# A seven-product matmul kernel on one core: the first loads spread over three DMA queues, the first matmuls narrower, and three small pieces of vector work cut in halves

## The chip, the cores and the metric

The kernel runs on one core of one Trainium2 chip. The metric is the device time of one execution in microseconds (us), the median of several runs. The core has five engines that run side by side, each through its own instructions in order: PE (TensorE, the matmuls; "PEld" in the profile is its loading of weights), DVE (VectorE), ACT (ScalarE), POOL (GpSimd) and SP (SyncE, which here only issues DMA transfers). SP, ACT and POOL each have a DMA queue. Operands lie in SBUF, matmul results in eight PSUM banks.

## What is computed

The input `x` is 1024 x 512, `weight` is 64 x 512 x 512, `lin_w` is 512 x 512. Cut to what matters:

```python
out_lin = x @ lin_w.T + lin_b
xv = jnp.einsum('bf,efm->bem', x, weight)
zp = jnp.einsum('bf,efm->bem', jnp.square(x), jnp.square(weight))
out = out_lin + 0.5 * jnp.sum(jnp.square(xv) - zp, axis=1)
```

Since the sum over e of `x^2 @ w_e^2` is `x^2 @ sum_e w_e^2`, the kernel needs one matmul of `x` with every `w_e`, whose result is squared and summed, and besides only sums of squares of the weights.

## The kernel before, in words

**The work.** Every matmul is done as seven products of blocks in place of eight (a Strassen-like scheme). `x` transposed is cut in four quads `A11, A12, A21, A22` (half of the batch by half of the features), and from them come seven left operands: `A11`, `A12`, `A22` themselves and `R5, R6, R7, R3`, which DVE makes as differences (`x_sum`, line 520). A right matrix is cut in quads too. The products carry the numbers 1 to 7; number 1 needs `A11`, number 2 `A12`, number 4 `A22`, number 5 `R5`.

**Stage one, the linear term** (lines 572 to 656). PE works through products 1, 2, 4, 5, 6, 3, 7 of `x` and `lin_w`, in plain fp32, four matmuls of 512 columns each (`one_level`). The right operands are the quads of `lin_w`, called `lw0` and `lw1` (row r) with column c 0 or 1, and four sums of them, `lt` 1 to 4 (`column_sums`, line 534): sum 1 is lw0 c0 + lw0 c1, sum 2 is sum 1 + lw1 c1, sum 3 is lw0 c1 + lw1 c1, sum 4 is lw1 c0 + sum 2. Product 4 takes sum 4, product 5 sum 1, product 6 sum 2, product 7 sum 3. In front of all that stand two matmuls of zeros (line 607): they need no load and keep PE at work from the start.

**The first loads** (lines 488 to 513). SP's queue brings `x` in pieces of 256 KB, each half a quad (k 0 or 1 of it): `A11` k 0 and 1, `A12` 0 and 1, `A22`, `A21`, then the bias. ACT's queue brings `lin_w`: `lw0` c0 in two pieces of 128 KB, `lw1` c0, `lw0` c1, `lw1` c1 in pieces of 256 KB. POOL's queue brings nothing then. Behind these stand the first weights on SP's queue. A piece is awaited by its own semaphore; there are eight for the transfers of SP and ACT, so a ninth transfer waits until the first has landed.

**Stage two, the weights** (from line 952). 32 blocks h of the weights, each with four quads `w11, w12, w21, w22` loaded as 512 KB, go through products 1, 6, 2, 3, 7, 5, 4. Each operand of a product is split into three pieces `H, L, K` (`split`, line 710), and a product is three passes of fp32r matmuls of 512 columns (line 782), with ACT, DVE and POOL making the pieces, adding, squaring and summing. For the sums of squares, ACT squares each weights' quad and DVE sums it (`w_squares`, line 703): one `ACTIVATE` and one `TENSOR_REDUCE` of 128 x 1024 for each. `IN_HALVES` (line 40) names the blocks whose `w21` is loaded as two transfers of 256 KB.

**Stage three** (from line 974) multiplies the squares of `x` with the sums of squares (line 936) and stores the result.

**The order.** No engine's order is written down. Every operation is entered in a plan (class `Plan`, line 84) with a cost on its engine, its reads and writes; loads have assumed times of landing (`landing`, line 485). PE's order is fixed by keys. `Plan.order` (line 180) lays out the others by how late each may come, in 60 rounds with random shifts, and the best round is emitted. So a changed cost or time of landing anywhere gives a new order of ACT, DVE, POOL and SP everywhere.

**Names in the listings.** `w11_1` holds `A11`, `w12_1` `A12`, `w22_1` `A22`, `sq_0` `A21`, `p5_0` `lw0`, `p1_1` `lw1`, `p5_1` the sums 1 and 2, `p5_2` the sums 3 and 4, `p1_0` `R5`, `w_0` `R7`, `sq_1` `R6`, `w_1` `R3` (the table `home`); the profile leaves the numbers out, so `xT` into `w` is a load of `A11`, `A12` or `A22`, and `lin_wT` into `p` one of `lin_w`. `X1H, X1L, X1K` and so on are the three pieces of a left operand.

## Time and profile before

| what | us |
|---|---|
| median of 3 runs | 1276.41 (1275.95 to 1278.27) |
| the profiled execution, time | 1276.26 |
| its span in the trace | 1274.4 |
| PE busy | 1270.1 |
| DVE, POOL, ACT busy | 1105.6, 1051.9, 1022.4 |

The span runs from the first to the last instruction in the trace; 1.86 us of the profiled execution's time lie outside it. The trace gives each instruction's start, its busy time, and, where its engine stood idle before it, what ended the wait; a group's row gives how many there are and the mean of one. "Us to landing" is from the start of the instruction that issues a transfer to the arrival of its last byte. A matmul of fp32 appears as two records and two loads of weights.

### The profile page before, as it was taken

How to read it: one execution, taken by the hardware profiler on the slowest of the kernel's cores; microseconds unless marked ns; L12 is line 12 of the kernel's file. 1: busy time of each engine (PE TensorE's matmuls, PEld its weight loads, DVE VectorE, ACT ScalarE, POOL GpSimd, SP SyncE). 2: the span in 40 equal slices, each digit the busy share in tenths (PEclk: the TensorE clock that was granted, in tenths of full speed). 3: DMA queues.
4: the chain of work that ended last, by engine and by line, in shares of the span. 5: the costliest groups of instructions: out<-in, count | busy, mean ns of one | idle time of the engine just before them, and what ended most of it. 6: DMA issues, size and time to landing. Idle time of an engine off the chain costs nothing.

```text
span 1274.4 us, 15633 instructions
## 1 busy us (share of the span) xinstructions
PE 1270.1 (100%) x5532; PEld 1036.8 (81%) x5532; DVE 1105.6 (87%) x959; ACT 1022.4 (80%) x1080; POOL 1051.9 (83%) x532
## 2 busy tenths in 40 slices
PE   9999999999999999999999999999999999999998
PEld 4888888888888888888888888888888888888887
DVE  6899998888888898888898888898888888888987
ACT  7788987788877788877788877788887788887991
POOL 2998898888898888898888898888888888888884
PEclk9999999999999999999999999999999999999999
DMA  8776655445655455655545655545654546665553
GB/s 247 191 167 168 136 107 141 120 96 141 149 109 143 120 119 130 153 114 135 128 98 131 149 115 141 140 102 123 154 123 125 134 99 139 149 127 126 141 123 101
DMA packets 69597, 170.49 MB, mean 134 GB/s; under 512 B 23088, under 2 KB 24880, under 8 KB 69520
## 3 DMA queue, kind: packets, MB, share of 16 engines
q0 software_dynamic: 20240, 72.49, 33.3%
q1 hardware_dynamic: 47744, 95.31, 22.7%
q10 hardware_dynamic: 1536, 1.70, 0.4%
q8 instruction: 43, 0.70, 0.2%
q14 instruction: 34, 0.28, 0.1%
HBM read 158.73 MB, written 8.13 MB: 131 GB/s over the span
## 4 chain that ended last, share of the span: by engine, by line
PE 100%; DVE 0%; DVEq 0%; issue 0%
PE bank L782 96%; PE bank L936 2%; PE bank L590 1%; PE bank L579 1%; PE bank L607 0%; DVE T L1027 0%; DVEq L1069 0%
## 5 line engine op out<-in xcount | busy, mean ns | idle before, releaser
L446 POOL TENSOR_TENSOR pK<-pH,pL 128x1024 fp32r<-128x1024 f32 x225 | 593.0, 2640 | 171.2 <-PE bank L782 160.9
L453 DVE TENSOR_REDUCE acc<-sq 128x16 f32<-128x1024 f32 x256 | 310.3, 1214 | 48.2 <-ACT sq L428 47.1
L428 ACT ACTIVATE sq<-bank 128x1024 f32<-128x1024 f32 x256 | 261.4, 1021 | 102.7 <-PE bank L782 64.8
L446 POOL TENSOR_TENSOR pL<-T,pL 128x1024 fp32r<-128x1024 f32 x95 | 257.7, 2713 | 2.8 <-DVE X5K L434 1.2
L434 DVE SCALAR_TENSOR_TENSOR bank<-bank,w 128x1024 f32<-128x1024 f32 x192 | 235.0, 1224 | 26.0 <-PE bank L782 25.8
L440 DVE TENSOR_TENSOR w<-bank,p 128x1024 f32<-128x1024 f32 x128 | 156.1, 1219 | 47.8 <-PE bank L782 47.4
L434 DVE SCALAR_TENSOR_TENSOR bank<-bank,p 128x1024 f32<-128x1024 f32 x128 | 154.0, 1224 | 25.9 <-ACT p L428 23.0
L446 POOL TENSOR_TENSOR pL<-w,pL 128x1024 fp32r<-128x1024 f32 x64 | 171.5, 2679 | 1.3 <-ACT pL L428 0.5
L428 ACT ACTIVATE pL<-T 128x1024 fp32r<-128x1024 f32 x95 | 100.4, 1057 | 68.7 <-issue 44.4
L453 DVE TENSOR_REDUCE w_sum<-wsq 128x16 f32<-128x1024 f32 x128 | 154.2, 1205 | 0.0
L428 ACT ACTIVATE wsq<-w 128x1024 f32<-128x1024 f32 x128 | 135.7, 1060 | 2.7 <-DVE w_sum L453 2.7
L428 ACT ACTIVATE bank<-bank 128x1024 f32<-128x1024 f32 x128 | 130.1, 1017 | 8.8 <-PE bank L782 8.8
L428 ACT ACTIVATE pH<-w 128x1024 fp32r<-128x1024 f32 x129 | 136.7, 1059 | 0.0
L428 ACT ACTIVATE p<-bank 128x1024 f32<-128x1024 f32 x128 | 127.2, 1024 | 0.7 <-PE bank L782 0.7
L465 POOL DMA_DIRECT2D T<-weight x94 | 99.2, 1071 | 7.8 <-POOL pL L446 7.8
L428 ACT ACTIVATE pL<-w 128x1024 fp32r<-128x1024 f32 x66 | 70.0, 1061 | 43.0 <-PE bank L782 24.1
L428 ACT ACTIVATE pH<-T 128x1024 fp32r<-128x1024 f32 x96 | 101.1, 1053 | 0.0
L434 DVE SCALAR_TENSOR_TENSOR pL<-pH,w 128x1024 fp32r<-128x1024 f32 x63 | 95.6, 1517 | 0.4 <-ACT pH L428 0.4
L782 PE MATMUL bank<-pH,X4H 128*128 128x512 f32 x256 | 79.6, 392 | 0.0
L782 PE MATMUL bank<-pH,X1H 128*128 128x512 f32 x256 | 79.2, 391 | 0.0
L782 PE MATMUL bank<-pL,X4L 128*128 128x512 f32 x256 | 79.0, 390 | 0.0
L782 PE MATMUL bank<-pL,X1L 128*128 128x512 f32 x256 | 78.8, 389 | 0.0
(148 smaller groups left out, 2515.9 us busy)
## 6 DMA issues: line engine op xcount, KB each, us to landing
w<-weight SPq DMA_DIRECT2D x114, 512.0 KB, 6.3
T<-weight POOLq DMA_DIRECT2D x94, 512.0 KB, 6.0
w<-weight POOLq DMA_DIRECT2D x32, 512.0 KB, 8.4
T<-weight SPq DMA_DIRECT2D x31, 512.0 KB, 4.5
w<-weight SPq DMA_DIRECT2D x28, 256.0 KB, 5.7
accd<-turned SPq DMA_DIRECT2D x60, 32.0 KB, 5.1
w<-xT SPq DMA_DIRECT2D x6, 256.0 KB, 4.9
lind<-accd POOLq DMA_DIRECT2D x3, 512.0 KB, 5.2
```

The lines of the kernel that those rows point to most:

```text
L428: nc.scalar.activation(o, i, func, bias=bias, scale=scale)
L434: return nc.vector.scalar_tensor_tensor(o, i, scalar, j, ALU.mult, op)
L440: return (nc.vector.tensor_sub if sub else nc.vector.tensor_add)(o, a, b)
L446: return (nc.gpsimd.tensor_sub if sub else nc.gpsimd.tensor_add)(o, a, b)
L453: lambda _: nc.vector.tensor_reduce(o, i.rearrange("p a (m e) -> p a m e", e=E), axis=AX.X, op=ALU.add),
L465: {POOL: 1.05}, lambda _: nc.gpsimd.dma_start(o, i, accum_op=ALU.add),
L579: return nc.tensor.matmul(buf[bank[u]], b[:, k, ts(u, P)], a[:, k, :], start=first and k == 0, stop=k == KH - 1, skip_group_check=True,)
L590: made = nc.tensor.matmul(buf[bank[u]], b[:, k, ts(u, P)], a[:, k, :], start=first and k == 0, stop=k == KH - 1, skip_group_check=True,)
L782: made = nc.tensor.matmul(buf[bank, j], buf[x][:, k, ts(2 * half + j, P)], buf[w][:, k, :], start=first and k == 0, stop=k == KH - 1, skip ...
L936: made = nc.tensor.matmul(buf[bank[u]], w[:, k, (2 * c + u) * P:(2 * c + u + 1) * P], x[:, k, :], start=fresh and z == 0 and i == which[0] ...
```

## The change

- `A11` k 1 and the whole of `A12` (512 KB, one transfer) go to POOL's queue. SP's queue has `A11` k 0, now in two transfers of 256 columns (128 KB each), then `lw0` c1, then `A22`, `A21` and the bias. ACT's queue has `lw0` c0, cut by columns u 0 and 1 (128 KB each, both k), then `lw1` c0 and c1.
- The four matmuls of product 1's first step (k 0; u 0 and 1) become four of 256 columns in place of two of 512, so that the first needs one half of `A11` k 0 and one half of `lw0` c0.
- Of the two matmuls of zeros the second has 256 columns in place of 512.
- Sums 2 and 4 are made in two halves (u 0 and 1) each, and sum 4 is entered ahead of sum 3.
- `w21`'s square and its sum are done in two halves for blocks 8 to 27, and blocks 12 and 13 join those whose `w21` is loaded in halves.
- The assumed times of landing are new, and with them the whole order.

```diff
-IN_HALVES = tuple((h, "w21") for h in range(14, 28))
+IN_HALVES = tuple((h, "w21") for h in range(12, 28))
+SUMS_IN_HALVES = tuple((h, "w21") for h in range(8, 28))
...
-    load_x("A11", 0, 4.2)
-    load_lw(nc.scalar, [0], 0, 4.3)
-    load_lw(nc.scalar, [1], 0, 5.1)
-    load_x("A11", 1, 5.9)
-    load_lw(nc.scalar, [2, 3], 0, 7.0)
-    load_x("A12", 0, 7.4)
-    load_lw(nc.scalar, [0, 1], 1, 8.8)
-    load_x("A12", 1, 8.5)
-    load_lw(nc.scalar, [2, 3], 1, 9.6)
+    load_x(nc.gpsimd, "A11", [1], 4.5)
+    load_x(nc.gpsimd, "A12", [0, 1], 6.8)
+    for z, at in enumerate((3.2, 4.0)):
+        nc.sync.dma_start(buf["A11"][:, 0, ts(z, H // 2)], x_src[:, 0, z * (H // 2):(z + 1) * (H // 2)])
+        landing(("A11", 0, z), at)
+        nc.scalar.dma_start(buf["lw0"][:, :, ts(z, P)], lw_src[:, :KH, ts(z, P)])
+        for k in range(KH):
+            landing(("lw0", k, 0, z), at + 0.2)
...
+    load_lw(nc.scalar, 1, 0, 5.8)
+    load_lw(nc.sync, 0, 1, 5.8)
+    load_lw(nc.scalar, 1, 1, 7.0)
     for at, (n, k) in enumerate((("A22", 0), ("A22", 1), ("A21", 0), ("A21", 1))):
-        load_x(n, k, 10.1 + 0.7 * at)
+        load_x(nc.sync, n, [k], 7.4 + 0.8 * at)
...
             (1, q[0, 0], q[0, 1], needs[0, 0] + needs[0, 1]),
             (2, t[1], q[1, 1], names[1] + needs[1, 1]),
+            (4, q[1, 0], t[2], needs[1, 0] + names[2]),
             (3, q[0, 1], q[1, 1], needs[0, 1] + needs[1, 1]),
-            (4, q[1, 0], t[2], needs[1, 0] + names[2]),
         ):
-            add(t[k], x, y, r, names[k])
+            if k in (1, 3):
+                dve(t[k], x, y, False, r, names[k], 512, True)
+                continue
+            for u in range(2):
+                o, x_u, y_u = (z[:, :, ts(u, P)] for z in (t[k], x, y))
+                reads = tuple(n for n in r if n[0] != "lt" or n[2] == u)
+                dve(o, x_u, y_u, False, reads, names[k][u:u + 1], 256, True)
...
+                if p == 1 and not k:
+                    for z in range(2):
+                        def emit(_, u=u, z=z):
+                            return nc.tensor.matmul(
+                                buf[bank[u]][:, ts(z, H // 2)], b[:, 0, ts(u, P)],
+                                a[:, 0, ts(z, H // 2)], start=first, stop=False,
+                                skip_group_check=True,
+                            )
...
-            plan.add({PE: 2 * WHOLE}, emit, a_names + b_names + (bank[u],), (bank[u],),
-                     key=key + 0.1 * u)
+            reads = a_names + tuple(n for n in b_names if n[0] != "lt" or n[2] == u)
+            plan.add({PE: 2 * WHOLE}, emit, reads + (bank[u],), (bank[u],), key=key + 0.1 * u)
...
-    for u in range(2):
+    for u, n in enumerate((N, N // 2)):
         nc.tensor.matmul(
-            buf[f2[u]], zero[:, 0:P], zero, start=True, stop=True, skip_group_check=True
+            buf[f2[u]][:, :n], zero[:, 0:P], zero[:, :n], start=True, stop=True,
+            skip_group_check=True,
         )
-    plan.add({PE: 3.4}, None, (), tuple(f2), key=-2000)
+    plan.add({PE: 3.3}, None, (), tuple(f2), key=-2000)
...
-        act(buf[sq], buf[n], AF.Square, (n,), (sq,))
         m = (h // NCB) * MG + (2 * col + h % NCB) * MI
-        reduce(w2_sum[:, ts(row, KH), m:m + MI], buf[sq], (sq,), (("w2", row, m),))
+        if (h, q) not in SUMS_IN_HALVES:
+            act(buf[sq], buf[n], AF.Square, (n,), (sq,))
+            reduce(w2_sum[:, ts(row, KH), m:m + MI], buf[sq], (sq,), (("w2", row, m),))
+            return
+        part = (sq, "second")
+        for k, reads, o in ((0, (n,), sq), (1, (n, sq), part)):
+            act(buf[sq][:, k], buf[n][:, k], AF.Square, reads, (o,), 512)
+        for k, reads in ((0, (sq,)), (1, (sq, part))):
+            at = row * KH + k
+            reduce(w2_sum[:, at:at + 1, m:m + MI], buf[sq][:, k:k + 1], reads, (("w2", row, m),), 512)
```

How the instructions stand on the engines is shown at three places. First SP, at the start of the program, before (`w11_1` is `A11`, `w12_1` `A12`, `w22_1` `A22`, `sq_0` `A21`, `p5_0` `lw0`):

```order
L490 DMA w11_1_87<-xT 128x512 x2
L490 DMA w12_1_89<-xT 128x512 x2
L490 DMA w22_1_92<-xT 128x512 x2
L490 DMA sq_0_104<-xT 128x512 x2
L512 DMA bias_121<-lin_b 128x4
```

and SP there after the change:

```order
L505 DMA w11_1_87<-xT 128x256 x2
L498 DMA p5_0_111<-lin_wT 128x2x256
L492 DMA w22_1_92<-xT 128x512 x2
L492 DMA sq_0_104<-xT 128x512 x2
L517 DMA bias_121<-lin_b 128x4
```

`A22`, fifth on SP's queue before, is now fourth, behind 512 KB in place of 1 MB; `A11` k 1 and `A12` have left the queue, and `lw0` c1 has come onto it from ACT's.

Second POOL, at the start of the program, before (`X2L` and `X2K` are pieces of `A12`, the additions are done by the transfers; `pK` is the first operand of the weights that POOL makes):

```order
L1062 MEMSET const-uint8-127 128x1
L1069 UNCONDITIONAL_BRANCH
L465 DMA X2L_69<-w12_1_89 128x1024
L465 DMA X2K_70<-X2L_69 128x1024
L446 ISA
L446 TENSOR_TENSOR pK_0_101<-pH_0_95,pL_0_98 128x1024
```

and POOL there after the change:

```order
L1094 MEMSET const-uint8-127 128x1
L1101 UNCONDITIONAL_BRANCH
L492 DMA w11_1_87<-xT 128x512
L492 DMA w12_1_89<-xT 128x2x512
L466 DMA X2L_69<-w12_1_89 128x1024
L466 DMA X2K_70<-X2L_69 128x1024
L447 ISA
L447 TENSOR_TENSOR pK_0_101<-pH_0_95,pL_0_98 128x1024
```

The loads of `A11` k 1 and of `A12` stand in front of what POOL's queue began with.

Third DVE, from its first instruction on, before (`p5_1` holds the sums 1 and 2, `p5_2` 3 and 4):

```order
L440 TENSOR_TENSOR X1L_66<-w11_1_87,X1H_65 128x1024
L440 TENSOR_TENSOR p5_1_112<-p5_0_111 128x512
L440 TENSOR_TENSOR p5_1_112<-p5_1_112,p1_1_108 128x512
L440 TENSOR_TENSOR p5_2_113<-p1_1_108,p5_1_112 128x512
L440 TENSOR_TENSOR p5_2_113<-p5_0_111,p1_1_108 128x512
L434 SCALAR_TENSOR_TENSOR X1K_67<-X1H_65,X1L_66 128x1024
L440 TENSOR_TENSOR p1_0_107<-w22_1_92,sq_0_104 128x1024
```

and DVE there after the change:

```order
L441 TENSOR_TENSOR X1L_66<-w11_1_87,X1H_65 128x1024
L441 TENSOR_TENSOR p5_1_112<-p5_0_111 128x512
L441 TENSOR_TENSOR p5_2_113<-p5_0_111,p1_1_108 128x512
L441 TENSOR_TENSOR p5_1_112<-p5_1_112,p1_1_108 128x2x128 x2
L441 TENSOR_TENSOR p5_2_113<-p1_1_108,p5_1_112 128x2x128 x2
L435 SCALAR_TENSOR_TENSOR X1K_67<-X1H_65,X1L_66 128x1024
L441 TENSOR_TENSOR p1_0_107<-w22_1_92,sq_0_104 128x1024
```

The rows are the sums in turn: 1, 2, 4, 3 before; now 1, then 3, then the halves of 2, then the halves of 4.

More of the change, by code (lines that the diff above doesn't have):

```diff
@@ L448, in pool, with reduce @@
         plan.add({POOL: 0.1 + 2.24 * size / 1024}, emit, reads, writes)
-    def reduce(o, i, reads, writes):
+    def reduce(o, i, reads, writes, size=1024):
         plan.add(
-            {DVE: 1.13},
+            {DVE: 0.06 + 1.07 * size / 1024},
             lambda _: nc.vector.tensor_reduce(
@@ L486, in landing, with load_x, load_lw @@
         plan.add({SP: 0.0}, None, (), (name,), land=at - 2 * plan.HOP)
[L488 removed]
+    def load_x(queue, n, ks, at):
         r, q = quads[n]
[L490 to L509 removed]
+        z = slice(q * KH + ks[0], q * KH + ks[-1] + 1)
+        queue.dma_start(buf[n][:, ks[0]:ks[-1] + 1], x_src[:, z, ts(r, H)])
+        for k in ks:
+            landing((n, k), at)
+    def load_lw(queue, n, c, at):
+        z = slice(KH * n, KH * n + KH)
+        queue.dma_start(buf[f"lw{n}"][:, :, ts(c, HM)], lw_src[:, z, ts(c, HM)])
+        for k in range(KH):
+            landing((f"lw{n}", k, c), at)
+    load_x(nc.gpsimd, "A11", [1], 4.5)
[4 more added lines that the diff above has]
+        nc.scalar.dma_start(buf["lw0"][:, :, ts(z, P)], lw_src[:, :KH, ts(z, P)])
+        for k in range(KH):
+            landing(("lw0", k, 0, z), at + 0.2)
+    for n in (("A11", 0), ("lw0", 0, 0), ("lw0", 1, 0)):
+        plan.add({NONE: 0.0}, None, ((*n, 0), (*n, 1)), (n,))
+    load_lw(nc.scalar, 1, 0, 5.8)
+    load_lw(nc.sync, 0, 1, 5.8)
+    load_lw(nc.scalar, 1, 1, 7.0)
     for at, (n, k) in enumerate((("A22", 0), ("A22", 1), ("A21", 0), ("A21", 1))):
[L511 removed]
+        load_x(nc.sync, n, [k], 7.4 + 0.8 * at)
     nc.sync.dma_start(bias[:], lin_b)
[L513 removed]
+    landing("bias", 10.4)
     nc.scalar.preload_act_table(AF.Square)
@@ L532, with column_sums @@
     }
-    def column_sums(q, t, needs, names, add):
+    def column_sums(q, t, needs, names):
         for k, x, y, r in (
@@ L577, in one_level @@
             for at, (u, k) in enumerate(steps):
+                if p == 1 and not k:
[6 more added lines that the diff above has]
+                            )
+                        plan.add({PE: WHOLE / 2}, emit, ((*a_names[0], z), (*b_names[0], u), bank[u]),
+                                 (bank[u],), key=key + 0.1 * at + 0.04 * z)
+                    continue
                 def emit(_, u=u, k=k):
```

20 lines of the change are left out of this document (4 added, 16 removed).

## The prediction

> **What bounds the kernel now.** The page first: the span, the busy times and the chain that ended last.
>
> ```profile
> span 1274.4 us, 15633 instructions
> PE 1270.1 (100%) x5532; PEld 1036.8 (81%) x5532; DVE 1105.6 (87%) x959; ACT 1022.4 (80%) x1080; POOL 1051.9 (83%) x532
> PE 100%; DVE 0%; DVEq 0%; issue 0%
> ```
>
> PE is busy in all but 4.3 us of the span, and the chain is PE alone. The change removes no matmul of real data. So it can act only where PE starts, or where PE waits between matmuls. Next come the waits in front of PE's loads of weights (us in total, times, longest):
>
> ```profile
> PEld bank L579 <- DMA p<-lin_wT: 1.9, 3, 1.4
> PEld bank L782 <- ACT sq L428: 1.1, 4, 0.4
> PEld bank L590 <- DVE p L440: 0.9, 2, 0.7
> ```
>
> PEld also idles 0.24 us in front of nearly every load while the matmul before runs, so even these rows overstate the loss. In the rest of the 1274 us nothing is to be won. The timeline of PE and its weight loads in the first 12 us:
>
> ```profile
> 0.77 3.75 PE L607 MATMUL bank<-const-float32-0.0 128*128 128x512 f32 x4 [0.77 <-PEq L1062]
> 1.76 0.34 PEld L607 LDWEIGHTS bank<-const-float32-0.0 128*128 128x128 f32 x1 [0.52 <-issue]
> 2.61 0.34 PEld L607 LDWEIGHTS bank<-const-float32-0.0 128*128 128x128 f32 x1 [0.52 <-issue]
> 4.38 0.45 PEld L579 LDWEIGHTS bank<-w,p 128*128 128x128 f32 x2 [1.43 <-DMA p<-lin_wT]
> 5.06 0.19 PEld L579 LDWEIGHTS bank<-w,p 128*128 128x128 f32 x1 [0.24 <-issue]
> 5.49 0.19 PEld L579 LDWEIGHTS bank<-w,p 128*128 128x128 f32 x1 [0.24 <-issue]
> 11.48 0.30 PEld L590 LDWEIGHTS bank<-w,p 128*128 128x128 f32 x2 [0.65 <-DVE p L440]
> 11.50 3.69 PE L590 MATMUL bank<-w,p 128*128 128x512 f32 x8
> ```
>
> A record of 512 columns takes 0.85 us among the zeros (1.76 to 2.61) and 0.43 later (5.06 to 5.49). The first real one took 5.06 - 4.38 = 0.68, so the speed doubled inside it, at about 4.9: 0.5 us at half speed and 0.18 at full make one record. The zeros' second record starts at 1.76, so they end at 1.76 + 3 x 0.85 = 4.31, and the first `lin_w` piece ended the wait at 4.38. A product is 8 records, 3.43 us: product 2 starts at 5.06 + 7 x 0.43 = 8.07, product 4 at 11.50, where the row stands. PE runs without a gap from 4.38 on, and what the front loses or gains moves the end by as much.
>
> **The loads.** Bytes by stage (last column GB/s, the one before it the DMA engines' busy share), then the answers for four single transfers (start of the issue, time to landing): `A11` k 0, `lw0` k 0, `A12` k 1, `lw1` c1.
>
> ```profile
> 0.00:2.00 2.00, 1.23 (x2) 0.74 (x3) 0.00 (x0) 0.00 (x0) 0.20 (x4) 1.00 0.13 20
> 2.00:4.00 2.00, 2.00 (x3) 0.43 (x2) 0.00 (x0) 0.00 (x0) 0.00 (x0) 1.00 0.88 241
> 4.00:6.00 2.00, 2.00 (x5) 0.91 (x5) 0.00 (x0) 1.24 (x1) 0.00 (x0) 1.00 1.02 350
> 6.00:8.00 2.00, 2.00 (x6) 0.87 (x5) 0.86 (x1) 1.15 (x3) 0.00 (x0) 1.00 1.07 375
> 8.00:10.00 2.00, 2.00 (x6) 0.95 (x5) 1.06 (x2) 2.00 (x3) 0.00 (x0) 1.00 1.07 389
> ```
>
> ```profile
> L490 SPq DMA_DIRECT2D w<-xT x1: 382/382/382, 0.7 to 0.7; - x1
> DMA to landing us min/median/max: 3.4/3.4/3.4
> ...
> L495 ACTq DMA_DIRECT2D p<-lin_wT x1: 415/415/415, 0.7 to 0.7; - x1
> DMA to landing us min/median/max: 3.6/3.6/3.6
> ...
> L490 SPq DMA_DIRECT2D w<-xT x1: 432/432/432, 2.1 to 2.1; - x1
> DMA to landing us min/median/max: 5.8/5.8/5.8
> ...
> L495 ACTq DMA_DIRECT2D p<-lin_wT x1: 375/375/375, 4.4 to 4.4; - x1
> DMA to landing us min/median/max: 5.6/5.6/5.6
> ```
>
> Two queues already keep the 16 DMA engines full from 2 us on (0.88, then over 1). Summed, 40 kB have moved by 2 us, 522 by 4, 1222 by 6, 1972 by 8, 2750 by 10 (a piece of 256 KB is 262 kB). The landings: 4.1 for `A11` k 0, 4.3 for `lw0` k 0, 7.9 for `A12` k 1, 10.0 for `lw1` c1. By 4.3 the pieces issued first make 262 + 131 = 393 kB, which the sum reaches at 2 + 353/241 = 3.46; by 7.9 `A11`, `A12` and `lin_w`'s c0 make 1572 kB, reached at 6 + 350/375 = 6.93. So a piece lands 0.9 us after the sum has reached all that was served up to it. This is my rule for what follows; what a transfer is served before or after is the unknown.
>
> **The change, part by part.**
>
> *Fewer zeros.* Three records in place of four end at 1.76 + 2 x 0.85 = 3.46. Alone this gives nothing, for the data of before come at 4.1 and 4.3.
>
> *First matmul.* It needs 131 + 131 kB, reached at 2 + 222/241 = 2.92, landed at 3.8. If POOL's `A11` k 1 is served among them, 524 kB and 4.9. I take 3.9. The clock is half until 4.9, so 0.48 us earlier is worth 0.24 us of work.
>
> *Rest of product 1.* `A11` and `lw0` c0, 786 kB: reached at 4 + 264/350 = 4.75, landed at 5.65. Then at most two half matmuls and two whole, 2.57 us, are left: product 1 ends by 8.2.
>
> *Product 2* needs `A12`, now one transfer with one landing, and `lw1` c0. Before, only `A12`'s first half was needed at 8.07. Needed bytes up to there: 1572 kB, and whatever else is served: SP's queue meanwhile has `lw0` c1 next (1834 kB), then `A22` k 0 (2097), and with `lw1` c1 and `A22` k 1 all of 2621. Landed: 7.8 with nothing else, 8 - 138/375 + 0.9 = 8.5 with `lw0` c1, 9.2 with `A22` k 0, 8 + 649/389 + 0.9 = 10.6 with everything. I take 8.5: before, the pieces of two queues landed in turn, and three queues in turn put just `lw0` c1 ahead. Against 8.07 that is 0.46 lost, and the 0.24 gained in front is eaten.
>
> The Trainium skill, in "DMA: Bandwidth & Descriptors", section "Issuing engines are not separate DMA queues", speaks against this part: transfers from all three queues run on the same 16 engines, and a further queue saves only time to issue. The DMA share of 1.02 to 1.07 here agrees; by the rule nothing lands earlier in sum, and if it were false the second rival below would hold.
>
> *The sums.* The vector instructions that make them, by form and from the timeline:
>
> ```profile
> L440 DVE TENSOR_TENSOR p<-p,p 128x512 f32<-128x512 f32 x3 | 2.0, 689 | 0.7 <-DMA p<-lin_wT 0.6
> L440 DVE TENSOR_TENSOR X6L<-sq,X6H 128x1024 fp32r<-128x1024 f32 x1 | 1.2, 1219 | 0.0
> 10.01 2.02 DVE L440 TENSOR_TENSOR p<-p,p 128x512 f32<-128x512 f32 x3 [0.62 <-DMA p<-lin_wT]
> ```
>
> Before, sum 2 starts with `lw1` c1 at 10.0, sum 4 follows, and product 4 starts at 11.5 with no time to spare. Now sum 3 comes first (0.69), then two halves of sum 2, then the first half of sum 4, which is enough for product 4's first half. No row shows 256 columns: at least half of 0.69, 0.345, at most 0.69. I take 0.42, from the line through 512 (0.689) and 1024 (1.219). `lw1` c1 lands with 2359 kB served (all of `A11`, `A12`, `lin_w`, and `A22` k 0) at 8 + 387/389 + 0.9 = 9.9; between 9.2 and 10.6 by the bounds above. Ready: 9.9 + 0.1 + 0.69 + 3 x 0.42 = 11.95; bounds 11.0 to 13.5. PE arrives at 8.53 + 3.43 = 11.96. So this costs nothing more, but it costs the same 0.46 if product 2 is in time: two waits stand in a row with one price. Behind on DVE, `X1K` (1.22) and `R5` (1.22) end at 11.95 + 0.42 + 2.44 = 14.8; product 5 wants `R5` at 11.96 + 3.43 = 15.4. What ACT has queued behind its first piece of `A12` moves by some 0.5 us; POOL's two new issues stand in front of an issue that idled 10 us. Nobody waits for either.
>
> *`w21`'s squares in halves.* Rows of whole ones, of a 512-column ACT instruction, and of one of the four PE waits of 0.4 us or less:
>
> ```profile
> L453 DVE TENSOR_REDUCE w_sum<-wsq 128x16 f32<-128x1024 f32 x128 | 154.2, 1205 | 0.0
> L428 ACT ACTIVATE wsq<-w 128x1024 f32<-128x1024 f32 x128 | 135.7, 1060 | 2.7 <-DVE w_sum L453 2.7
> 12.69 0.67 ACT L428 ACTIVATE wsq<-bank,bias 128x512 f32<-128x512 f32 x1
> 1016.71 1.03 ACT L428 ACTIVATE sq<-bank 128x1024 f32<-128x1024 f32 x1 [1.05 <-DVE w L440]
> ```
>
> 20 blocks: 20 x (2 x 0.67 - 1.06) = 5.6 us on ACT and 20 x (2 x 0.69 - 1.21) = 3.4 on DVE, over some 760 us in which ACT idles 20% and DVE 13%: hidden. If that cover failed, it would be 0.3 us a block. The PE waits at L782 are for a bank that ACT's square of a product frees, and that square found ACT idle for 1.05, waiting for DVE. Halves of other squares do not shorten that, so I take 0. Bounds: -1.1, all four waits gone, to +1.1, as many new ones, since the whole order is drawn again.
>
> **Sum.** Against the profiled execution (1276.26; span 1274.4 and 1.86 around it; 0.15 under the median of the runs): 1276.26 + 0.46 + 0 = 1276.7. A measurement of this kernel can tell about 0.2%, 2.55 us, from no change.
>
> **Rivals.**
>
> *The loads come as the plan assumes* (first pieces 3.2 and 3.4, `A12` 6.8, `lw1` c1 7.0). Then PE starts at 3.5, zeros permitting, runs 1.4 us at half speed in place of 0.5, and is 0.45 ahead for good: 1275.8. Against it: by 7.0 the assumed pieces make 2097 kB, and the trace had moved 1222 + 375 = 1597. For it: the 2 to 4 us stage ran at only 241 GB/s, where another mix might do better.
>
> *`A12` ends last: slower.* It is the second transfer of a queue that starts with 256 KB more, and POOL's transfers land late beside full queues:
>
> ```profile
> X2L<-w POOLq DMA_DIRECT2D x1, 512.0 KB, 9.7
> X4L<-w POOLq DMA_DIRECT2D x1, 512.0 KB, 4.6
> ```
>
> The first of these was issued at 10.5 while SP's weights streamed. Issued at about 1.7, `A12` would land between 6.3 and 11.4 by these; past 8.5 every us of delay is a us of PE. From 9.2 (+1.1, 1277.4) it reaches to 11.4 (+3.3, 1279.6); over 10.6 it decides for slower by more than 0.2%. Its middle is 1278.4. Against it: those two add into SBUF, and an addition reads twice.
>
> *The clock.* The speed doubled some 4.1 us after PE's first matmul, in a stretch without a gap. Now PE stands still between 3.46 and 3.9, and again while pieces come. If the doubling comes another such stretch later, up to 4.1 us run at half speed: 2.0 us at most, less what PE would wait anyway; about 1277.7. The Trainium skill, "TensorE: Matmul & The Clock Gate", section "Part 1: The HAM clock gate", has a free-running window of 3.4 us that must be busy; by that the loss is at most 1.7, and it can fall on any run, before or after.
>
> **How the numbers follow.** Forecast 0.50 (own range 1276.0 to 1277.6: the halves' price and 0.7 either side at `lw1` c1, waits of L782). Plan's loads 0.20. `A12` last 0.22, of which 0.08 over 10.6. Clock 0.08. Range 1275.3 to 1278.8: it takes in the plan's loads with half of the L782 waits gone, and leaves out the last part of the third queue's case and about as much below. Slower by over 0.2% (1279.0): 0.08 and 0.01 from the clock. Faster by over 0.2% would need 1273.9, below every gain in the rows together: 0.01. Same: 0.90.
>
> **What would show it.** Right: the weight load in front of product 2 waits for `xT` or `lin_wT` and starts at about 8.5; product 4 starts near 12.0, its wait ended by DVE; stage two is 0.5 us later than before. Wrong: product 2 at 7.6 with no wait (the plan's loads), or after 9.2 with `xT` as releaser (`A12` last); records of 0.85 us past 5 us (the clock); or waits at L782 that sum to more than 1 us over those of before.

## The result, and the profile after

The changed kernel takes 1279.99 us (median of 11 runs, 1278.55 to 1280.66) against 1276.14 us for the kernel before in the same comparison (1275.85 to 1278.27). The ratio, which compares means, is 1.0026, with a 95% interval of 1.0017 to 1.0034, so it is 2.2 to 4.3 us slower. The forecast was 1276.7 us in a range of 1275.3 to 1278.8, and the result lies outside it. The profiled execution took 1280.54 us. Its page:

```profile
span 1278.8 us, 15708 instructions
PE 1270.1 (99%) x5536; PEld 1037.6 (81%) x5536; DVE 1137.7 (89%) x981; ACT 1026.8 (80%) x1100; POOL 1052.1 (82%) x534
PE 96%; DVE 2%; DMA 2%; issue 0%; ACTq 0%; DVEq 0%
```

PE is busy for the same 1270.1 us, and the span is 4.4 us longer. The chain that ended last is no longer PE alone: 2% of it is DMA and 2% DVE. The waits of PE itself between 4 and 90 us (in all, times, longest) name the places:

```profile
PE bank L814 <- DMA X4K<-X4L: 1.4, 1, 1.4
PE bank L602 <- DMA p<-lin_wT: 1.3, 1, 1.3
PE bank L591 <- DMA p<-lin_wT: 1.1, 2, 0.6
PE bank L814 <- DVE p L441: 0.5, 1, 0.5
```

The two rows of L591 and L602 are products 1 and 2 waiting for loads. The two of L814 lie in the weights' stage, which the forecast left as it was: one waits at 75.6 us for a transfer of GpSimd's queue, the other at 35 us for an addition on DVE. The timeline shows the start (L591 are the 256-column matmuls: the two matmuls of product 1's first step are now four; L602 are the other matmuls of products 1 and 2, L613 product 4):

```profile
0.78 2.90 PE L630 MATMUL bank<-const-float32-0.0 128*128 128x512 f32 x4 [0.78 <-PEq L1094]
4.11 1.82 PE L591 MATMUL bank<-w,p 128*128 128x256 f32 x4 [0.43 <-DMA p<-lin_wT]
6.56 1.13 PE L591 MATMUL bank<-w,p 128*128 128x256 f32 x4 [0.63 <-DMA p<-lin_wT]
7.53 1.88 PE L602 MATMUL bank<-w,p 128*128 128x512 f32 x4
10.66 0.30 PEld L602 LDWEIGHTS bank<-w,p 128*128 128x128 f32 x2 [2.08 <-DMA w<-xT]
12.51 2.03 DVE L441 TENSOR_TENSOR p<-p,p 128x512 f32<-128x512 f32 x5 [2.40 <-DMA p<-lin_wT]
14.26 1.12 PE L613 MATMUL bank<-w,p 128*128 128x512 f32 x2
```

Product 1 stops from 5.93 to 6.56 for the second half of `lw0` c0. Product 2 starts at 10.7 (8.07 before). Its weight load was released by `xT`, which is `A12` (its last byte came at 10.36), and its first matmul by `lw1` c0, which landed 0.2 us after that, at 10.55. Sum 3 starts at 12.51, when `lw1` c1 is there (before, sum 2 started with it at 10.0), and product 4 starts at 14.26 (11.50 before): 2.76 us are lost by then, against the first trace of before. The loads by stage, with the same columns as before (the last is GB/s, the one ahead of it the DMA engines' busy share):

```profile
0.00:2.00 2.00, 1.22 (x2) 0.73 (x3) 0.00 (x0) 0.00 (x0) 0.92 (x6) 1.00 0.06 10
2.00:4.00 2.00, 1.68 (x3) 0.44 (x2) 0.00 (x0) 1.21 (x1) 0.76 (x2) 1.00 0.95 261
4.00:6.00 2.00, 1.82 (x4) 1.17 (x4) 0.00 (x0) 0.08 (x1) 0.00 (x0) 1.00 0.83 254
6.00:8.00 2.00, 1.44 (x6) 1.10 (x7) 0.00 (x0) 0.81 (x1) 0.00 (x0) 1.00 1.03 351
8.00:10.00 2.00, 1.41 (x4) 0.34 (x2) 1.72 (x2) 0.25 (x1) 0.00 (x0) 1.00 1.05 401
```

From 4 to 6 us only 254 GB/s moved, where it was 350 before. What moved between 7 and 9 us, when product 2 was waiting, by queue (q0 is GpSimd's, q1 SP's, q10 ACT's; packets, MB, share of the engines' time):

```profile
q0 software_dynamic: 112, 0.44, 56.1%
q1 hardware_dynamic: 118, 0.20, 29.8%
q10 hardware_dynamic: 121, 0.12, 18.0%
```

In this stretch the three queues had nearly equal numbers of packets, but GpSimd's are of 4 KB, so it had 56% of the time. `lw1` c0, which product 2 needs as well as `A12`, was on ACT's queue with 18%. In the same stretch of before, run again (an experiment below), ACT's queue moved 0.44 MB in place of 0.12:

```profile
q10 hardware_dynamic: 454, 0.44, 62.2%
q1 hardware_dynamic: 190, 0.33, 45.2%
```

These two queues did not have equal numbers of packets, so equal turns by packet are no rule that the traces bear out.

The wait at 75.6 us is on the transfer that makes `X4K`. It is issued at 65.1 and takes 12.1 us. Before it was issued at 52.7 and took 4.8.

```profile
L466 POOL DMA_DIRECT2D X4K<-X4L x1: 1166/1166/1166, 65.1 to 65.1; - x1
DMA to landing us min/median/max: 12.1/12.1/12.1
  PE bank L814: 1.4, 1
```

To account for the whole program, each trace's PE matmuls were matched with those of the first trace of before, one to one from the last backwards. The difference of the starts at a place is what was lost up to there. For the changed kernel that is +2.76 at product 4, +2.37 more up to 100 us (0.7 at 35 us, 1.6 at 75.6; counted from product 4's second record), -0.98 between 100 and 1240 us, +0.14 behind. The first trace of before turns out below to have had an early start. Against its second trace, the loss is 1.1 at product 4, 2.4 up to 100 us, -0.6 up to 1240 us and 0.2 behind: 3.1 us in all, near the 3.3 of the ratio.

### The profile page after: what moved, and what is told of

The parts are those of the page before. It is cut to its first block, busy times and chain, and to the rows that moved or that the text cites. A ratio compares the mean times of both kernels' runs of the same rounds, so it can differ in the third digit from the quotient of the medians.

```text
span 1278.8 us, 15708 instructions
## 1 busy us (share of the span) xinstructions
PE 1270.1 (99%) x5536; PEld 1037.6 (81%) x5536; DVE 1137.7 (89%) x981; ACT 1026.8 (80%) x1100; POOL 1052.1 (82%) x534
## 4 chain that ended last, share of the span: by engine, by line
PE 96%; DVE 2%; DMA 2%; issue 0%; ACTq 0%; DVEq 0%
PE bank L814 93%; PE bank L968 1%; PE bank L613 1%; DMA X4K<-X4L 1%; DMA p<-lin_wT 1%; DVE bank L435 0%; DVE w L441 0%; DVE acc L454 0%; PE bank L602 0%; DVE T L441 0%; DVE p L441 0%; DVE p L435 0%; DVE sq L441 0%; DVE pL L435 0%; ACTq L507 0%
## 5 line engine op out<-in xcount | busy, mean ns | idle before, releaser
L447 POOL TENSOR_TENSOR pL<-T,pL 128x1024 fp32r<-128x1024 f32 x95 | 254.7, 2681 | 0.6 <-ACT pL L429 0.2
L429 ACT ACTIVATE wsq<-w 128x1024 f32<-128x1024 f32 (+1 forms) x148 | 138.1, 940 | 25.1 <-DVE w_sum L454 25.1
L454 DVE TENSOR_REDUCE w_sum<-wsq 128x16 f32<-128x1024 f32 (+1 forms) x148 | 157.0, 1061 | 0.0
L435 DVE SCALAR_TENSOR_TENSOR pL<-pH,w 128x1024 fp32r<-128x1024 f32 x63 | 124.2, 1971 | 6.2 <-ACT pH L429 6.1
L466 POOL DMA_DIRECT2D T<-weight x94 | 94.6, 1006 | 9.4 <-POOL pL L447 7.8
L814 PE MATMUL bank<-pH,X5H 128*128 128x512 f32 x256 | 78.9, 389 | 0.5 <-DVE p L441 0.5
L814 PE MATMUL bank<-pH,X1H 128*128 128x512 f32 x256 | 79.2, 391 | 0.0
L814 PE MATMUL bank<-pH,X4H 128*128 128x512 f32 x256 | 79.0, 390 | 0.0
L814 PE MATMUL bank<-pL,X4L 128*128 128x512 f32 x256 | 78.9, 389 | 0.0
```

Of the source, the lines that this page charges most:

```text
L429: nc.scalar.activation(o, i, func, bias=bias, scale=scale)
L435: return nc.vector.scalar_tensor_tensor(o, i, scalar, j, ALU.mult, op)
L447: return (nc.gpsimd.tensor_sub if sub else nc.gpsimd.tensor_add)(o, a, b)
L454: lambda _: nc.vector.tensor_reduce(o, i.rearrange("p a (m e) -> p a m e", e=E), axis=AX.X, op=ALU.add),
L466: {POOL: 1.05}, lambda _: nc.gpsimd.dma_start(o, i, accum_op=ALU.add),
L814: made = nc.tensor.matmul(buf[bank, j], buf[x][:, k, ts(2 * half + j, P)], buf[w][:, k, :], start=first and k == 0, stop=k == KH - 1, skip ...
```

## The experiments

The kernels e1 to e6, e8, e9 (no e7 was run) and f1 to f3 keep the changed kernel's plan, so that no engine's order moves except for the named edit; before with the loads keeps before's in the same way. Before with the half sums and with the half squares, and the three draws, have orders of their own. The table has, for each, the ratio of its time to that of before in the same comparison with its 95% interval, and from its trace the start of product 4 and the loss in three stretches, matched as above.

| run | ratio (interval) | product 4 at | from there to 100 us | 100 to 1240 us | at the end |
|---|---|---|---|---|---|
| first trace of before | | 11.50 | 0 | 0 | 0 |
| before again | 1.0002 (0.9993 to 1.0010) | 13.14 | -0.01 | -0.37 | +1.25 |
| changed | 1.0026 (1.0017 to 1.0034) | 14.26 | +2.37 | -0.98 | +4.31 |
| e1, two queues | 1.0016 (1.0007 to 1.0024) | 13.65 | +1.13 | -0.95 | +2.51 |
| e2, X4's places | 1.0023 (1.0014 to 1.0033) | 14.07 | +0.63 | -0.43 | +2.84 |
| e3, full zeros | 1.0037 (1.0023 to 1.0050) | 14.43 | +1.58 | -0.42 | +4.13 |
| e4, whole squares | 1.0039 (1.0026 to 1.0051) | 14.20 | +0.73 | +0.23 | +3.72 |
| e5, two queues, uncut | 1.0017 (1.0008 to 1.0027) | 13.56 | +1.46 | -0.96 | +2.76 |
| e6, three queues, uncut | 1.0023 (1.0013 to 1.0032) | 15.08 | +0.72 | -0.72 | +3.63 |
| e8, two queues, `lw0` cut | 1.0013 (1.0003 to 1.0022) | 12.61 | +1.04 | -0.96 | +1.35 |
| e9, two queues, `A11` cut | 1.0018 (1.0008 to 1.0027) | 12.82 | +0.93 | -0.91 | +1.51 |
| before with the loads | 1.0023 (1.0014 to 1.0032) | 14.75 | -0.04 | -0.61 | +2.53 |
| before with the half sums | 1.0025 (1.0015 to 1.0035) | 13.01 | +0.03 | +1.88 | +3.62 |
| before with the half squares | 1.0007 (0.9998 to 1.0015) | 12.91 | -0.01 | -0.14 | +1.25 |
| f1, three old places | 1.0022 (1.0013 to 1.0031) | 14.75 | -0.01 | -0.54 | +2.79 |
| f2, old places, old loads | 1.0005 (0.9996 to 1.0014) | 13.88 | -0.01 | -0.64 | +1.85 |
| f3, old places, late piece on GpSimd | 1.0004 (0.9995 to 1.0013) | 12.90 | +0.05 | -0.57 | +0.91 |
| before, draw 1 | 1.0030 (1.0018 to 1.0041) | 12.25 | +1.89 | +1.47 | +4.53 |
| before, draw 2 | 1.0004 (0.9995 to 1.0013) | 13.17 | +0.29 | -0.34 | +2.07 |
| before, draw 3 | 1.0032 (1.0020 to 1.0045) | 12.74 | +1.04 | +1.71 | +4.58 |

The theories at first were L, that the third queue's loads delay the products, and O, that the new orders of DVE and GpSimd made the waits at 35 and 75 us. Each of the first four kernels undoes one part of the change.

**e1, the changed kernel with its loads on two queues.** The pieces stay cut as in the change, in the order in which they are needed. `load_x` and `load_lw` now only tell the plan the old assumed landings; the transfers are issued behind them:

```diff
+    def load_x(queue, n, ks, at):
+        for k in ks:
+            landing((n, k), at)
...
     load_x(nc.gpsimd, "A11", [1], 4.5)
     load_x(nc.gpsimd, "A12", [0, 1], 6.8)
...
+    x_piece(nc.sync, "A11", 1)
+    lw_piece(nc.scalar, 1, 0)
+    x_piece(nc.sync, "A12", 0)
+    lw_piece(nc.scalar, 0, 1)
+    x_piece(nc.sync, "A12", 1)
+    lw_piece(nc.scalar, 1, 1)
...
```

> The changed kernel with only the first loads issued otherwise: nothing on POOL's queue; SP has A11 k 0 (two halves), A11 k 1, A12 k 0 and 1, A22, A21; ACT has lw0 c0 (two halves), lw1 c0, lw0 c1, lw1 c1. The plan and so the order on every engine stay as in the changed kernel. Theory L (the loads in three queues made product 2 wait): product 2 starts at 8.0 to 8.3 us in place of 10.69; product 4 then waits for the sums (lw1 c1 at 9.9, then 0.69 and three halves of 0.34), 11.7 in place of 14.26; the front gives back about 2.5 us. If the waits at 35 us and at 75 us stay, the time is 1277.5; if they shrink with the front, 1276.5. Rival N (the narrower matmuls, fewer zeros or halved sums lost the front): product 2 no earlier than 10, no gain, 1280.

Product 4 came at 13.65, only 0.6 us earlier than in the changed kernel, and the ratio is 1.0016. Theory L in this form missed: even on two queues the start was 2.2 us later than in before's trace. What holds the loads back there was the next question.

**e2, X4L and X4K back in their old places on GpSimd.** In the order that the plan gives, X4L is put behind the first of GpSimd's sums of pieces and X4K behind the seventh.

```diff
-    for op, engine in plan.order():
+    done = plan.order()
...
+    for piece_name, place in (("X4L", 0), ("X4K", 6)):
+        i = next(i for i, (o, e) in enumerate(done) if o.n == marks[piece_name])
+        moved_op = done.pop(i)
...
+        done.insert(i + 1, moved_op)
```

> The changed kernel with only the two transfers that make X4L and X4K put back to where they stood on POOL in the kernel before (behind its first and its seventh sum of pieces); all else in its order. Theory O (the new order put them late): the PE wait for X4K at 75.6 us (1.55 and 0.08) goes, span 1277.2, time 1.6 less than the changed kernel, 1278.4. Rival Q (X4K is late because the front was late and the DMA queues are full at that time, 12.1 us to landing): the wait shrinks by less than half, time 1279.5 or more.

X4K's transfer takes 5.5 us in place of 12.1 to land, and PE's wait for it is gone. The waits of PE from 4 to 90 us that are left:

```profile
PE bank L606 <- DMA w<-xT: 2.1, 2, 1.2
PE bank L818 <- DVE p L441: 0.4, 1, 0.4
```

So the wait at 75 us, 1.6 us in the changed kernel's trace, came of where two instructions stand. The 1.6 us that theory O gave for the time is not shown: the ratio hardly moved (1.0023 against 1.0026), which the intervals allow, for they are 2 us wide, and the place is worth only 0.2 to 1.6 us in the traces that kept it.

**e3, the second matmul of zeros whole again.**

```diff
-    for u, n in enumerate((N, N // 2)):
+    for u, n in enumerate((N, N)):
```

> The changed kernel with only the second matmul of zeros back at 512 columns. Theory L: product 2 waits for its loads to 10.7 whatever happened before, so no change, 1280.0 give or take 0.4, though PE's records reach 0.43 us per 512 columns earlier than at 5.5 us. Rival C (the clock, doubling later because PE stood still, is part of the 2.76 us): 0.5 us or more are won.

Nothing was won: product 4 came at 14.43, and the ratio, from four runs, is if anything higher (1.0037). That the shorter zeros cost something isn't seen.

**e4, w21's square and sum whole again in the changed order.**

```diff
-            act(buf[sq][:, k], buf[n][:, k], AF.Square, reads, (o,), 512)
+            def emit(_, k=k):
+                return None if k else nc.scalar.activation(buf[sq], buf[n], AF.Square, bias=0.0, scale=1.0)
...
```

> The changed kernel with the squares of w21 and their sums done whole, at the places where the plan has the first half of the square and the second half of the sum; the order of all else is unchanged. Theory H (the halves removed the four waits for PSUM banks between 712 and 1137 us, 0.5 us in sum): such waits come back, 0.5 us more, 1280.5. Rival R (the order as drawn anew removed them): no such waits, same time as the changed kernel, 1280.0.

From 130 to 1250 us the weight loads wait 11 times for ACT's squares; in the changed kernel they never do, and in before four times:

```profile
PEld bank L824 <- ACT sq L429: 2.3, 11, 0.4
```

Theory H is right in kind, though the waits come back at other places: the four of before, between 712 and 1137 us, stay gone, as they do in every other order that was drawn, with whole squares too. Between 100 and 1240 us this kernel loses 0.23 us where the changed one gains 0.98. So in the changed order the halves were worth 1.2 us in the trace; the ratios, 1.0039 and 1.0026, agree in sign, and their intervals overlap.

The second four asked what kept the start late on two queues: the cuts (theory C), or something else in the new program (theory S).

**e5, the changed kernel with before's loads exactly,** and **e6, its three queues without the cuts.**

```diff
+    x_piece(nc.sync, "A11", 0)
+    for k in range(KH):
+        lw_row(nc.scalar, k)
...
-        nc.sync.dma_start(buf["A11"][:, 0, ts(z, H // 2)], x_src[:, 0, z * (H // 2):(z + 1) * (H // 2)])
...
-        nc.scalar.dma_start(buf["lw0"][:, :, ts(z, P)], lw_src[:, :KH, ts(z, P)])
...
```

> The changed kernel with the first loads of before (two queues, A11 k0 whole, lw0 c0 in its two k rows of 1 KB, before's order), all else as changed. If the cut pieces keep some of the 16 DMA engines behind (theory C), the engines' lag is gone, A11 k1 lands by 5.8, lw1 c0 by 8.2, lw1 c1 by 10.3, product 4 starts by 12.0 and the time falls by 1.5 to 2.3 us beside the changed kernel's 1280.0, to about 1278. If something else in the new program keeps them behind (theory S: the later start of the matmuls, the table load or the program's own fetches), product 4 stays at 13.5 to 14.3 and the time at 1279 to 1280.

> The changed kernel's three queues, with A11 k0 whole and lw0 c0 in k rows of 1 KB: the third queue without the cuts. Theory C: no lagging engines, product 4 at 12.0 to 12.6 (GpSimd's 4 KB packets of A12 still ahead of lw1), time about 1278. Theory L (the third queue takes the turns of the queues with what is needed first): product 2 still at 10.0 or later, product 4 at 13.5 or later, time 1279 to 1280.

**e8 and e9, two queues with one of the two cuts each** (the lines above for `lw0`, or for `A11`, as in e1).

> Two queues in before's order, A11 k0 whole, only lw0 c0 cut by columns (512-byte rows, two loads of 256 descriptors). If the short rows of lw0 are the cut that costs (theory C1), engines lag and product 4 starts at 13.3 or later; if it is the cut of x or the whole count of loads ahead (theory C2), product 4 is within 0.4 of e5's.

> Two queues in before's order, lw0 c0 in k rows of 1 KB, only A11 k0 cut in halves of 256 columns (two loads of 1 KB rows). C1: product 4 within 0.4 of e5's; C2: engines lag and product 4 starts at 13.3 or later. In both the first matmul starts by 4.2.

Theory C fell: e5, with the very loads of before, still started product 4 at 13.56, which lies in theory S's range, and e8 and e9, with one cut each, were not later but earlier. The three queues were again the latest without any cut (15.08). That left S, or the first trace of before as an unusual one. The next four kernels start from the kernel before.

**Before again, unchanged.**

> The kernel before, unchanged, once more: a control for the start. Theory V (in the first 6 us one DMA engine or another is held up to 1 us by a single packet, in every kernel, by chance): A11 k1's last completion differs from the first profile's 5.56 by 0.3 us or more, and product 4 starts between 11.5 and 12.8. Theory N (before's start is steady and the lag belongs to the changed kernel): last completions within 0.2 us of the first profile's, product 4 at 11.4 to 11.6. The time is before's in both, within 0.6 us.

Its time is that of before (1.0002), but its product 4 starts at 13.14. PE's waits from 4 to 90 us, which the first trace did not have, and the timeline:

```profile
PE bank L590 <- DVE p L440: 0.7, 1, 0.7
PE bank L579 <- DMA p<-lin_wT: 0.5, 1, 0.5
```

```profile
8.75 3.70 PE L579 MATMUL bank<-w,p 128*128 128x512 f32 x8 [0.53 <-DMA p<-lin_wT]
11.67 2.02 DVE L440 TENSOR_TENSOR p<-p,p 128x512 f32<-128x512 f32 x3 [1.53 <-DMA p<-lin_wT]
13.14 2.41 PE L590 MATMUL bank<-w,p 128*128 128x512 f32 x5 [0.69 <-DVE p L440]
```

So before itself waits for `lw1` c0 and then, through the sums, for `lw1` c1. Both theories missed with their numbers: product 4 is later than the 12.8 of theory V, and `A11` k 1 (5.29 against 5.56) is not late; the pieces behind it are. What holds of theory V is that before's start differs from trace to trace, and theory N is out. The first trace had caught an early start. Six traces of the kernel before with its own loads (unchanged, with half sums, with half squares, and in three other orders) have product 4 at 12.25 to 13.17.

The landings of `lw1` c1 decide on theory S. Its last byte came at 9.9 in the first trace of before and at 10.7 to 11.8 in the other six, at 11.8 in e5 and 11.5 in f2, which have before's loads in the changed program, and at 10.2 to 11.9 in e1, e8 and e9. In the seven traces that have `A11` k 1 and `A12` on a third queue it came at 12.1 to 12.7. So the changed program by itself doesn't make the loads later; the third queue does, with the cuts or without.

In before, product 4 starts 1.6 us after that last byte in all six traces with whole sums. In the changed kernel, e1, e5 and e9, where the sums are what it waits for, it is 1.8, because the drawn order does sum 3 first. In before with the half sums, below, where sum 3 comes last, it is 1.25. So the halves work, and the order that the planner drew gave more than their gain away.

**Before with the changed first loads alone.**

```diff
+    x_piece(nc.gpsimd, "A11", [1])
+    x_piece(nc.gpsimd, "A12", [0, 1])
+    for z in range(2):
+        nc.sync.dma_start(buf["A11"][:, 0, ts(z, H // 2)], x_src[:, 0, z * (H // 2):(z + 1) * (H // 2)])
+        nc.scalar.dma_start(buf["lw0"][:, :, ts(z, P)], lw_src[:, :KH, ts(z, P)])
+    lw_piece(nc.scalar, 1, 0)
+    lw_piece(nc.sync, 0, 1)
+    lw_piece(nc.scalar, 1, 1)
```

> The kernel before with the first loads of the changed kernel alone (three queues, A11 k0 and lw0 c0 in halves by columns); zeros, matmuls, sums, squares and every order as before. Theory Q (the third queue with its 4 KB packets is what delays lw1): lw1 c0 last at 9.5 or later, product 4 at 13.2 to 14.3, the time 1.5 to 2.8 us over before's. Theory M (the 256-column matmuls and the halves of the sums are what costs at the start): product 4 by 12.2, the time within 0.7 us of before's.

Theory Q holds, with a later start than it gave: product 2 waits 2.1 us and starts at 11.21, and product 4 at 14.75. Here `A12` lands last (11.17), after `lw1` c0 (10.30). Nothing is lost afterwards. The interval of the ratio is 1.8 to 4.1 us.

```profile
11.21 3.70 PE L594 MATMUL bank<-w,p 128*128 128x512 f32 x8 [2.07 <-DMA w<-xT]
12.35 2.02 DVE L440 TENSOR_TENSOR p<-p,p 128x512 f32<-128x512 f32 x3 [2.35 <-DMA p<-lin_wT]
```

**Before with the half sums alone.** Its plan is drawn anew, as the change's is.

```diff
+            for u in range(2):
+                o, x_u, y_u = (z[:, :, ts(u, P)] for z in (t[k], x, y))
+                reads = tuple(n for n in r if n[0] != "lt" or n[2] == u)
+                dve(o, x_u, y_u, False, reads, names[k][u:u + 1], 256, True)
```

> The kernel before with the two sums of lin_w in halves and their new order alone; the order that follows on DVE, ACT and GpSimd is another one too (L12's add comes after the next sum of pieces, X4L and X4K are issued later). Theory O (the new orders cost, wherever the loads are): product 4 within 0.4 us of before's 11.5, then a wait of 0.4 to 0.7 at 35 us, one of 0.3 to 1.6 at 75 us, the time 0.6 to 2.2 us over before's. Rival: these waits came of the late start alone, and the time is within 0.4 us of before's.

The start is no later than that of before, run again (13.01 against 13.14), there is no wait at 35 or 75 us, and still it is 1.0025. The loss between 100 and 1240 us is 1.88 us, most of it in 22 small steps from 141 to 1036 us: two of 0.25 us where PE waits for ACT's squares, the others of 0.04 to 0.11. The half sums end at 14 us, so it can't be they. Only the order is left, and theory O was right in kind and wrong in place.

The other twenty lie at one place of a block, the first weight load of product 6's pass `K`. The rows there, in this kernel and then in before, run again:

```profile
236.12 2.35 DVE L434 SCALAR_TENSOR_TENSOR bank<-bank,p 128x1024 f32<-128x1024 f32 x2
237.46 0.76 PEld L787 LDWEIGHTS bank<-pK,X6K 128*128 128x128 f32 x4 [0.23 <-issue]
```

```profile
234.76 1.22 DVE L434 SCALAR_TENSOR_TENSOR bank<-bank,p 128x1024 f32<-128x1024 f32 x1
237.00 0.87 PEld L782 LDWEIGHTS bank<-pK,X6K 128*128 128x128 f32 x4
```

The profile gives no releaser, since an instruction of PE's queue that does nothing but wait stands in front of the load. That instruction ends 0.09 us after DVE's addition into a PSUM bank does (the first of the two in the row, at 237.34), in all 20 of these stops. In before, run again, the addition had ended at 235.98, a full microsecond ahead of the load.

**Before with w21's squares in halves alone,** from the change.

> The kernel before with W21's squares in halves alone (reads in halves from block 12, squares from block 8). Theory H (the halves take PE's waits at 712, 1022, 1098 and 1136 us away and cost nothing else): 0.4 to 0.8 us under before's time. Rival: the waits stay or move, within 0.2 us of before's; or new waits on the longer DVE and ACT work, up to 0.5 us over.

No gain: 1.0007. The four waits at 713 to 1136 us are gone, as in every newly drawn order, and others come (869, 907, 984, 1171 us).

The last six were made for what was still open: whether the loads and the named places are all of the loss, whether a third queue costs by itself, and what a new order costs by itself.

**f1 and f2.** f1 is the changed kernel with X4L, X4K and the second half of L12's addition in the places that they have before; f2 has before's loads as well (e5).

```diff
+    for n, after in ((marks["X4L"], sums_of_pieces[0]), (marks["X4K"], sums_of_pieces[6]), (marks["L12"], None)):
+        moved_op = done.pop(place_of(n))
+        moved_op[0].after = None
+        done.insert(place_of(marks["L22"]) if after is None else place_of(after) + 1, moved_op)
```

> The changed kernel, its loads kept, with three operations put back where before has them: X4L and X4K on GpSimd, the second half of L12's add on DVE. Theory A (loads, X4K's place and L12's place are all of the loss): no waits at 35 and 75 us, product 4 at 14.0 to 14.4, the time 1.5 to 2.6 us over before's. Rival (the waits move elsewhere): the time stays 3 us or more over before's.

> As f1, and with before's loads on two queues, uncut. Theory A: nothing of the loss is left; product 4 at 12.8 to 13.6 as in the other profiles with before's loads, the time within 0.6 us of before's, rather under than over it (the waits at 712 to 1136 us are gone). Rival (256-column matmuls, half sums or shorter zeros cost by themselves): 0.8 us or more over before's.

Between product 4 and 100 us both traces lose nothing (-0.01). f1 keeps the ratio of the loads alone, 1.0022; f2 comes to 1.0005 (-0.5 to +1.8 us), which can't be told from before. Product 4 is later than theory A gave in both (14.75 and 13.88). So the loads and three instructions' places make up what can be measured of the loss; up to 1.8 us for the rest can't be excluded by f2 alone.

**f3, as f2 with `lw0` c1, needed late, on GpSimd's queue.** The edit is against f2; the line also moves to the front of the loads.

```diff
-    lw_piece(nc.scalar, 0, 1)
+    lw_piece(nc.gpsimd, 0, 1)
```

> As f2, but lw0 c1, first needed for the sums ahead of product 4, goes by GpSimd's queue instead of ScalarE's. Theory W (the third queue costs by carrying early what is needed late, in large packets): lw0 c1 lands early, lw1 c1 as late or up to 0.5 us earlier, the time within 0.6 us of f2's. Theory Q (a third queue costs by itself): lw1 c1 at 12.2 or later, product 4 at 14.0 or later, 1.0 us or more over f2.

Theory W: the sums start with `lw1` c1 at 10.7 (11.54 in f2), and the ratio is 1.0004. So a third queue by itself costs nothing that can be told; it costs when it carries 768 KB early. GpSimd's packets are of 4 KB here too, so their size alone is not the cause. Whether 768 KB of something needed late would cost as much was not tried.

```profile
9.37 3.70 PE L634 MATMUL bank<-w,p 128*128 128x512 f32 x8 [1.17 <-DMA p<-lin_wT]
10.72 2.03 DVE L441 TENSOR_TENSOR p<-p,p 128x512 f32<-128x512 f32 x5 [1.36 <-DMA p<-lin_wT]
12.90 2.31 PE L645 MATMUL bank<-w,p 128*128 128x512 f32 x5
```

**Three other draws of the kernel before.** Nothing but the number that starts the planner's random shifts is changed; all instructions are the same.

```diff
-    SEED = 0
+    SEED = 1
```

> The kernel before with nothing changed but the number that starts the planner's random shifts: ACT, DVE, GpSimd and SP run in another order, with the same instructions. GpSimd issues X4L after four more sums and X4K after six more. Theory D (a new draw of the order costs by itself, as in the kernel with half sums alone): 0.6 to 3.5 us over before's, with small waits spread over blocks or a wait for X4K at 72 to 76 us. Rival (orders that the planner rates alike run alike): within 0.4 us of before's.

> The kernel before with a second other start of the planner's random shifts; its order on GpSimd and SP is near before's (X4L and X4K stay in their places), on DVE and ACT it differs. If before's order is an unusually good draw: 1 to 4 us over before. If the first other draw was an unusually bad one: within 0.8 us of before.

> The kernel before with a third other start; its order differs on every engine but PE, as in the first other draw. If before's order is an unusually good draw: 1 to 4 us over before. If the first other draw was an unusually bad one: within 0.8 us of before.

Draws 1 and 3 cost 3.8 and 4.1 us by their ratios, as much as the whole change. Draw 2, which leaves X4L and X4K in their places, costs nothing that can be told. So one of three other draws is as good as before's. In draw 1 the weight loads of L782 stop 27 times for nothing that the profile names, 6.4 us in all, and twice for DVE:

```profile
PEld bank L782 <- issue: 6.4, 27, 0.9
PEld bank L782 <- DVE p L440: 0.9, 1, 0.9
PEld bank L782 <- DVE w L440: 0.5, 1, 0.5
```

```profile
PEld bank L782 <- issue: 0.5, 2, 0.2
```

The first fence is draw 1; the second is before again, with two such stops. They are the stops of the half-sum kernel: between 100 and 1240 us, 23 in draw 1 and 21 in draw 3 stand in front of the first load of product 6's pass `K`, each behind a wait-only instruction that ends 0.09 us after DVE's addition. There are none in before, draw 2 and the changed kernel. No version was found that is faster than the kernel before: the best, f3, has an interval of 0.9995 to 1.0013.

## Why the prediction was wrong

**The loads' rule was made from one early start.** "A piece lands 0.9 us after the sum has reached all that was served up to it" fitted a trace whose product 4 started at 11.50, where the same kernel's other traces lie at 12.25 to 13.17. The forecast's sum had PE arriving at product 4 with no time to spare and the loads just ahead of it. In the second trace of before the loads are already what ends last, and there each us by which `lw1` c1 is later is a us of PE. It put the last byte of `lw1` c1 at 9.9 with the change; it came at 12.5, and in before's six later traces at 10.7 to 11.8. The step also took 350 GB/s for the stage from 4 to 6 us; it was 254.

**What the third queue is served before: mis-sized.** I took 8.5 for product 2, with only `lw0` c1 ahead of its pieces, because "three queues in turn put just `lw0` c1 ahead". The bound for "everything" was 10.6, and the trace has 10.7. From 7 to 9 us GpSimd's queue had 56% of the engines' time and ACT's, with `lw1` c0, 18%. The lateness sits in a few of the 16 DMA engines: the sixteen completions of `lw1` c0 in the changed kernel's trace run from 6.53 to 10.55 us, the eighth at 7.3; in before's second trace from 6.34 to 8.71. The product needs the last.

**The rival "`A12` ends last" came true in the front.** Its row was a weight load of product 2 after 9.2 with `xT` as releaser: it is there, 2.08 us at 10.66. Product 4's 2.76 us are inside the +1.1 to +3.3 that it gave. That is in part luck: before's own second trace is 1.65 us later than the start from which these were counted. `A12` was not alone in being last either: `lw1` c0 landed 0.2 us after it in the changed kernel's trace, and 0.9 us ahead of it in before with the loads. The measured 1279.99 lies above the rival's 1279.6, since the waits in stage two come on top. It had 0.22 where it deserved more than the forecast.

**Drawing the order again: the step that failed outright.** I wrote "so I take 0. Bounds: -1.1, all four waits gone, to +1.1, as many new ones, since the whole order is drawn again", and looked for new waits only among those that existed. The runs show that a draw by itself costs from nothing to 4.1 us. In the changed kernel it put two waits of 0.7 and 1.6 us at 35 and 75 us, both at places where before has no wait at all, and f1 removed both by moving three instructions. Its own sign for this, waits in stage two of more than 1 us over before's, is there. The four old waits did go, worth 0.5 us in the trace.

**What held.** Fewer zeros gave nothing (e3). The first matmul came at 4.11 (3.9 forecast). The halves of the sums took 0.42 each, as forecast, but each began 0.335 after the one before, so the chain of sums was shorter than its sum in the forecast. The halves of the squares cost 2.9 us on DVE (3.4 forecast), and no loss by them can be told: +0.9 us with an interval of -0.3 to +1.9, in an order of its own.

**The clock** was a true rival of its own in some runs. The profile's granted clock reads 1.00 in all of these stages, so only the records tell. In f2 the eight records of 256 columns took 3.78 us and in f3, with the same code, 1.99:

```profile
4.20 3.78 PE L623 MATMUL bank<-w,p 128*128 128x256 f32 x8 [0.52 <-DMA p<-lin_wT]
7.77 6.28 PE L634 MATMUL bank<-w,p 128*128 128x512 f32 x12
```

```profile
4.26 1.99 PE L623 MATMUL bank<-w,p 128*128 128x256 f32 x8 [0.58 <-DMA p<-lin_wT]
```

The first fence is f2, the second f3. By the spacing of the records the speed doubled at 4.9 us in before's first trace, by 4.3 in f3's, between 5.6 and 6.6 in the changed kernel's, where PE stood still in between, and at about 9.7 in f2's. There it is worth some 0.6 us by this estimate: the sums started at 11.54, and with the changed kernel's 1.75 us from there (12.51 to 14.26) product 4 could have started at 13.3 in place of 13.88. The Trainium skill, "TensorE: Matmul & The Clock Gate", section "Part 1: The HAM clock gate", has the full clock come after a busy window of about 3.4 us, sustained, and the window runs free. That the doubling comes late where PE had stood still for 0.5 us agrees with this in f2, but f3 stood still for 0.6 us and had doubled by 4.3; the runs do not settle when it comes.

**What stays open.** How much of the 3.3 us of the ratio is the loads and how much the places can't be told closer than about 1 us: the loads alone are 2.9 on before (1.8 to 4.1), while e5, without them, is at 2.2 (1.0 to 3.4), and the parts together exceed the whole. What puts DVE's addition behind in the half-sum kernel and in draws 1 and 3 was not followed up. No draw was timed for the changed kernel, so what another order of it would take is not shown.

## What to carry to other kernels

Where a planner sets the order, any edit, even one of cost zero, is also a new draw: price it by other draws of the kernel before, and judge an edit with the order held still. One trace of a start that waits on loads is one sample; take a second before you build a rule on its landing times. An additional queue should carry only what is needed last, since it takes its share of the DMA engines from the start on. Where a row names no releaser, look for an instruction in front of it that only waits, and for what ended just before that.
